# A four-layer graph network: transposed count blocks by transposing DMA transfers in place of a second matrix, and edge weights computed in slices inside attention

## The chip, the cores and the metric

The kernel runs on one core of one Trainium2 chip. The core has five engines with their own instruction streams: TensorE (PE, with its weight loads as PEld), VectorE (DVE), ScalarE (ACT), GpSimd (POOL) and SyncE (SP), which here issues DMA transfers; POOL issues the indirect ones. The metric is the device time of one launch in microseconds (us), given as the median of some runs; a profile describes one further, separately recorded execution.

## The reference

There are 3125 nodes with 256 features and 50,000 directed edges, sorted by destination. Four stages follow one another, and after each one its result is added to its input and normalized over the features (`x = layernorm(x + layer(x))`):

- Layer 0: an input projection and two transformer layers whose attention runs over the edges (8 heads of 32, softmax over the edges of each destination) with a feed-forward part of width 1024.
- Layer 1: graph attention with 4 heads of 64. An edge's weight is `exp(leaky_relu(el[src] + er[dst]))`, summed per source.
- Layer 2: two hypergraph convolutions. Each multiplies by a weight, sums over the edges from sources to destinations, divides by the destination's number of edges, and sums back from destinations to sources.
- Layer 3: messages along the edges. Each message is multiplied by four edge attributes and by a radial weight of the edge, which needs only the edge's ten length features and two small weights, nothing of the layers before:

```python
h = silu(edge_len_emb @ fc_w1 / np.sqrt(10.0)) * SILU_NORM     # 10 -> 64
msg_rad = h @ fc_w2 / np.sqrt(64.0)                            # 64 -> 1
messages = msg_ang * msg_rad
agg = segment_sum(messages, edge_dst, num_segments=n)
```

## The kernel before

Nodes are padded to NP = 3200, that is NN = 25 tiles of P = 128. Edges are laid out as NT = 391 columns of 128. The class `Sorted` holds the path that runs; a fallback for inputs that are not sorted stands in the other branch of a test and is not run.

**The count matrix.** Layers 1 and 2 don't walk over edges: they multiply by a dense 3200 x 3200 bfloat16 matrix in HBM that holds how many edges go from a source to a destination. Two of them are made. `mats[0]` has a row for each destination and a column for each source, `mats[1]` the other way round. Each is zeroed by 20 transfers of 1 MB (`clear`, L1117) and then filled by 391 indirect transfers on POOL, each writing 128 two-byte counts to places given by `put0` or `put1` (`fill`, L1131, for `mats[0]`; `fill_now`, L1138, for `mats[1]`). `count`, `put0` and `put1` are made in the prologue (`counts`); `put1` goes to HBM by L1112 and is read back in layer 1.

**Prologue** (`prepare`, from 0 to about 286 us). It finds each tile's edges, tests the order, makes the counts, and in `project_all` goes over the 25 tiles: input projection, store of h (L1272), one `clear` of `mats[0]` for each of the first 20 tiles, normalization, and query, key and value rows with their stores (L1245, L1248); the tile's edge lists (L1023, L1024, with a value read into a register of SP) come some tiles later. The radial weights of layer 3 are here too. `load_edge_weights` loads the ten features of all edges, fc_w1 six times on a diagonal, fc_w2, and the four attributes (`attr`). `edge_weights` then takes 66 steps: a float32 matmul over six groups of 128 edges (L1918, two passes on PE), Silu on ACT (L1921), a product and a sum on DVE (L1922, L1923). At the end it multiplies `attr` by the result (L1925), transposes 16 blocks (L1930), copies them (L1932) and stores them as e_w (L1933). Then `put_by` stores six tables to HBM as by_* (L1033), and the next stage begins with loading them as k_* (`fetch_by`, L1039).

**Attention** (`attend`, once for each of the two layers of layer 0; about 290 to 1226 and 1233 to 2134 us). For each tile of destinations 17 indirect gathers of key and value rows run on POOL (recorded at the helper line L996), one gather of scores (`mine`, L996) and five fills of `mats[0]`; on PE the query rows are spread over the edges (L1467), and values are summed (L1543). SP and POOL keep the order in which the code is written (the class `InOrder`). In attention layer 0 each of the first 20 tiles also issues one `clear` of `mats[1]`. Groups of GP = 3 tiles are handed to `feed`, a generator with the output, feed-forward (L1325, L1339) and next projection (L1384). Generators stand in a list `work`; `pump(n)` advances the first of them by n yields, so that feed work lies between the pieces of attention. At the end of attention layer 1, POOL issues the fills of `mats[0]` that are left.

**Layer 1** (`layer1`, 2134 to about 2765 us). For blocks of 1280, 1280 and 640 sources and two pairs of heads it loads rows of `mats[0]` as m1 (L1765), makes edge terms on ACT and DVE (L1768, L1770) and multiplies on PE (L1774). After each tile's products, `fill_now` issues four fills of `mats[1]` on POOL until all 391 are issued. After each block an epilogue (transposes L1786, DVE, ACT) normalizes and splits each float32 feature into three bfloat16 parts (`split`).

**Layer 2** (`layer2`, to about 3735 us). `conv` is called four times: with `mats[1]` and `parts` from source to destination (first and third), with `mats[0]` and `mids` back (second and fourth). A conv goes over five groups c of CT = 5 output tiles and, for each, over 25 input tiles b. For each b it loads a 128 x 640 block of the matrix as m2 (L1820, 160 KB, eight buffers), whose five 128 x 128 pieces are the weights of ten matmuls (L1825, L1827). In the first conv ACT also sums each block's rows (`tally`, L1852) for the number of edges of each source. **Layer 3** gathers rows and applies e_w to the end at 4357.7 us.

Of the kernel before, what the change touches and what calls it, by code (L numbers as in the profile page):

```python
# [8 lines left out]
F32 = mybir.dt.float32  # L9
I32 = mybir.dt.int32  # L10
# [44 lines left out]
RU = 6  # L55
LATE = 4
RS = 1280
FILL, FILL1 = 5, 4
# [944 lines left out]
class Sorted(General):  # L1003
# [58 lines left out]
    def counts(self, k, cp, sp, raw):  # L1062
# [6 lines left out]
        self.put1 = self.dram.tile([P, NT], I32, name="put1d")  # L1069
# [34 lines left out]
        back = cp.tile([P, NT], F32, name="back")  # L1104
        nc.vector.scalar_tensor_tensor(back, src, float(NP), d, op0=ALU.mult, op1=ALU.add)
        put1 = cp.tile([P, NT], I32, name="put1s")
        for c, to in ((code, self.put0), (back, put1)):
            gap = sp.tile([P, NT], F32, name="gap")
            nc.vector.tensor_sub(gap, behind, c)
            nc.vector.tensor_mul(gap, gap, away)  # L1110
            nc.vector.tensor_add(to, gap, c)
        nc.sync.dma_start(self.put1, put1)  # L1112

    def clear(self, i, z, c):

        rows = self.mats[i][:NP * NP, :].rearrange("(p c) o -> p (c o)", p=P)
        ins = self.tc.nc.sync.dma_start(rows[:, c * ZC:(c + 1) * ZC].rearrange("p (r z) -> p r z", z=ZB),  # L1117
                                        z[:, None, :].to_broadcast([P, ZC // ZB, ZB]))
        self.tc.keep_in_program_order(ins)

    def zeros(self):
        z = self.keep.tile([P, ZB], BF16, name="zmat")
        self.nc.vector.memset(z, 0.0)
        self.mats = [self.dram.tile([NP * NP + EP, 1], BF16, name=f"mat{i}") for i in range(2)]
        return z

    def fill(self, i, put, j, behind):

        tc = self.tc
        with tc.issue_after(behind.ins):  # L1130
            ins = tc.nc.gpsimd.indirect_dma_start(  # L1131
                out=self.mats[i], out_offset=bass.IndirectOffsetOnAxis(ap=put, axis=0),
                in_=self.count[:, j:j + 1], in_offset=None)
        tc.declare_no_dep(ins.ins, group=f"fill{i}", reason="each place is written once")
        tc.add_to_no_dep_group(f"fill{i}", ins.ins)

    def fill_now(self, i, put, j):
        ins = self.tc.nc.gpsimd.indirect_dma_start(  # L1138
            out=self.mats[i], out_offset=bass.IndirectOffsetOnAxis(ap=put[:, j:j + 1], axis=0),
            in_=self.count[:, j:j + 1], in_offset=None)  # L1140
        self.tc.declare_no_dep(ins.ins, group=f"fill{i}", reason="each place is written once")
        self.tc.add_to_no_dep_group(f"fill{i}", ins.ins)
# [118 lines left out]
    def project_all(self, w, xs, wi, b, z, sp, ip, pp, mp, beside):  # L1261
# [3 lines left out]
        for t in range(NN):  # L1265
# [7 lines left out]
            if t < NP * NP // P // ZC:  # L1273
                self.clear(0, z, t)
# [126 lines left out]
    def attend(self, l, qw):  # L1401
# [6 lines left out]
        with ExitStack() as at:  # L1408
# [48 lines left out]
            def scores(t):  # L1457
# [25 lines left out]
                for c in range(FILLED[l] + t * FILL, FILLED[l] + (t + 1) * FILL):  # L1483
                    self.fill(0, self.put0[:, c:c + 1], c, behind)
                if l == 0 and t < NP * NP // P // ZC:
                    self.clear(1, self.z, t)
# [80 lines left out]
            def put(t, y_p):  # L1567
# [4 lines left out]
                if len(group) == GP or t == NN - 1:  # L1572
                    work.append(self.feed(s.hs, list(group), w, nxt, sp, hp, tp, mp))
                    group.clear()
# [9 lines left out]
            for t in range(NN + 2):  # L1584
# [31 lines left out]
                for c in range(FILLED[l] + NN * FILL, FILLED[l + 1] if t == NN else 0):  # L1616
                    self.fill(0, self.put0[:, c:c + 1], c, behind_all[0])
# [10 lines left out]
                members(t + 1)  # L1628
            pump(1000)
# [27 lines left out]
    def layer0(self, qw):  # L1657
# [4 lines left out]
        for i in range(2):  # L1662
            t = self.dram.tile([CAP + P, H], F32, name=f"scores{i}")
            nc.sync.dma_start(t[CAP:, :], z)
            self.scores.append(t)
        nxt = self.attend(0, qw)
# [12 lines left out]
    def layer1(self, parts):  # L1679
# [7 lines left out]
        mat = self.mats[0][:NP * NP, :].rearrange("(d s) o -> d (s o)", s=NP)  # L1687
        with ExitStack() as at:
# [10 lines left out]
            put1 = cp.tile([P, NT], I32, name="put1")  # L1699
            nc.sync.dma_start(put1, self.put1)  # L1700
# [47 lines left out]
            fills = iter(range(0, NT, FILL1))  # L1748
            for s0 in range(0, NP, RS):
                R = min(RS, NP - s0)  # L1750
                ot = op.tile([A1, H1, RS], F32, name="ot")
                for h0 in range(0, H1, 2):
# [6 lines left out]
                    for t in range(NN):  # L1759
# [16 lines left out]
                        j = next(fills, NT)  # L1776
                        for j in range(j, min(j + FILL1, NT)):
                            self.fill_now(1, put1, j)
# [29 lines left out]
    def conv(self, mat, parts, mp, ap, seen, done):  # L1808
# [3 lines left out]
        mat = mat[:NP * NP, :].rearrange("(d s) o -> d (s o)", s=NP)  # L1812
# [419 lines left out]
```

## Time and profile before

| | us |
|---|---|
| median of three runs | 4371.66 |
| the three runs | 4358.33, 4371.66, 4374.93 |
| the profiled execution | 4359.61 |
| its span in the trace | 4357.7 |
| PE busy | 3706.8 (85%) |
| DVE busy | 2609.1 (60%) |
| POOL busy | 2406.7 (55%) |
| ACT busy | 1360.6 (31%) |

The span is what the trace covers; the profiled execution's own time is 1.9 us longer. TensorE was granted 0.911 of its clock on average. A page's slices cut the span into 40 equal parts and give each engine's busy share in tenths; the windows give the same for stretches that one chooses, in us; the waits say which engine stood for whom, with the total, the number and the longest. A line number such as L1138 is a line of the code above; a DMA queue's own instructions have SPq for SP and POOLq for POOL.

### The profile page before, as it was taken

How to read it: one execution, taken by the hardware profiler on the slowest of the kernel's cores; microseconds unless marked ns; L12 is line 12 of the kernel's file. 1: busy time of each engine (PE TensorE's matmuls, PEld its weight loads, DVE VectorE, ACT ScalarE, POOL GpSimd, SP SyncE). 2: the span in 40 equal slices, each digit the busy share in tenths (PEclk: the TensorE clock that was granted, in tenths of full speed). 3: DMA queues.
4: the chain of work that ended last, by engine and by line, in shares of the span. 5: the costliest groups of instructions: out<-in, count | busy, mean ns of one | idle time of the engine just before them, and what ended most of it. 6: DMA issues, size and time to landing. Idle time of an engine off the chain costs nothing.

```text
span 4357.7 us, 53699 instructions
## 1 busy us (share of the span) xinstructions
PE 3706.8 (85%) x18807; PEld 2534.5 (58%) x18912; DVE 2609.1 (60%) x5129; ACT 1360.6 (31%) x2336; POOL 2406.7 (55%) x2116
## 2 busy tenths in 40 slices
PE   5866888888866888878799999299999999799998
PEld 3434666666645666666433334166556655688887
DVE  6956787787647787776467768211222123566665
ACT  3720222232211223223467768355111111000000
POOL 0026777777677777777788887600000000477776
PEclk8957988998967999989799999699999999899999
DMA  7847777776266666663222222133333333233333
GB/s 177 223 151 204 210 230 214 211 218 194 67 194 183 184 191 180 184 198 111 85 76 64 70 61 60 27 90 90 94 101 89 90 105 115 75 99 100 97 99 88
DMA packets 362289, 577.13 MB, mean 132 GB/s; under 512 B 85417, under 2 KB 265380, under 8 KB 361949
## 3 DMA queue, kind: packets, MB, share of 16 engines
q1 hardware_dynamic: 246186, 286.55, 23.1%
q0 software_dynamic: 115824, 287.06, 22.6%
q8 instruction: 152, 2.49, 0.2%
q14 instruction: 127, 1.04, 0.1%
HBM read 486.46 MB, written 86.91 MB: 132 GB/s over the span
## 4 chain that ended last, share of the span: by engine, by line
PE 34%; POOL 30%; issue 9%; DVE 9%; DMA 7%; ACT 1%; SPq 1%; POOLq 0%; ACTq 0%; DVEq 0%
POOL mat L1138 13%; PE cv L1825 11%; POOL g L92 10%; PE cv L1827 6%; POOL mat L1131 4%; PE qe L1467 4%; PE mm L1339 3%; PE acc L1543 3%; POOL kv L996 3%; PE mm L1325 3%; DMA kv<-kv,k_src 3%; DMA mine<-scores,row 2%; DVE kv L1541 1%; PE w_p L1860 1%; PE mm L1384 1%
## 5 line engine op out<-in xcount | busy, mean ns | idle before, releaser
L996 POOL DMA_INDIRECT kv<-kv,k_src x850 | 843.7, 993 | 538.7 <-issue 225.6
L92 POOL DMA_INDIRECT g<-l_tab,k_src x425 | 469.9, 1106 | 1055.5 <-issue 1050.9
L1138 POOL DMA_INDIRECT mat<-k_count,put x391 | 564.3, 1443 | 119.2 <-issue 119.2
L1774 PE MATMUL acc<-e,xe 128*65 128x512 f32 (+2 forms) x1600 | 559.7, 510 | 36.9 <-DVE e L1770 21.5
L1131 POOL DMA_INDIRECT mat<-k_count,k_put x391 | 463.1, 1185 | 120.3 <-issue 112.2
L1467 PE MATMUL qe<-q,oht 128*128 128x256 bf16 x2550 | 392.7, 303 | 151.9 <-DVE kv L1469 111.0
L1770 DVE SCALAR_TENSOR_TENSOR e<-e,m 128x1280 f32<-128x1280 f32 (+1 forms) x300 | 379.2, 1268 | 168.3 <-ACT e L1768 148.6
L1543 PE MATMUL acc<-kv,oh 128*128 128x264 f32 x1700 | 441.5, 418 | 33.1 <-DVE kv L1541 32.2
L1825 PEld LDWEIGHTS <-m 128*128 128x128 bf16 x2500 | 244.8, 98 | 361.0 <-issue 75.5
L1467 PEld LDWEIGHTS <-oht 128*128 128x128 bf16 x2550 | 319.7, 146 | 228.0 <-issue 159.5
L1774 PEld LDWEIGHTS acc<-e,xe 128*65 128x65 f32 x1600 | 216.7, 141 | 368.7 <-issue 308.4
L1768 ACT ACTIVATE e<-el,l_one,fr 128x1280 f32<-128x1280 f32 (+1 forms) x300 | 380.7, 1275 | 160.6 <-PE acc L1774 159.4
L1543 PEld LDWEIGHTS acc<-kv,oh 128*128 128x128 f32 x1700 | 347.7, 209 | 110.8 <-DVE kv L1541 45.4
L1827 PE MATMUL cv<-parts,m 128*128 128x256 bf16 x1250 | 338.8, 273 | 76.5 <-DMA m<-mat 73.9
L1825 PE MATMUL cv<-mids,m 128*128 128x512 bf16 x1199 | 394.4, 379 | 10.6 <-DVE y L1847 9.7
L1825 PE MATMUL cv<-parts,m 128*128 128x512 bf16 x1196 | 396.5, 380 | 0.3
L1469 DVE TENSOR_TENSOR kv<-kv,qe 128x512 f32<-128x512 f32 (+1 forms) x450 | 285.9, 651 | 168.3 <-DMA kv<-kv,k_src 86.6
L1981 DVE TENSOR_TENSOR ws<-oh,w_n 128x512 f32<-128x512 f32 x425 | 291.7, 691 | 158.3 <-PE acc L1986 152.2
L1986 PEld LDWEIGHTS acc<-g,ws 128*128 128x128 f32 x2550 | 352.9, 192 | 22.2
L1986 PE MATMUL acc<-g,ws 128*128 128x128 f32 x2550 | 354.4, 275 | 0.0
L1827 PE MATMUL cv<-mids,m 128*128 128x256 bf16 x1250 | 338.8, 273 | 2.6
L1983 PE MATMUL acc<-g,ws 128*128 128x256 f32 x850 | 265.1, 394 | 51.2 <-DMA g<-l_tab,k_src 39.3
(296 smaller groups left out, 5259.8 us busy)
## 6 DMA issues: line engine op xcount, KB each, us to landing
m<-mat SPq DMA_DIRECT2D x550, 160.0 KB
mat<-zmat SPq DMA_DIRECT2D x40, 1000.0 KB
m<-mat SPq DMA_DIRECT2D x100, 320.0 KB
keys<-e_dst SPq DMA_DIRECT2D x50, 544.0 KB
q<-q SPq DMA_DIRECT2D x100, 192.0 KB
kv<-kv,k_src POOLq DMA_INDIRECT x850
kv<-qkv SPq DMA_DIRECT2D x50, 256.0 KB
g<-l_tab,k_src POOLq DMA_INDIRECT x425
```

The source lines that it names most:

```text
L92: return self.nc.gpsimd.indirect_dma_start(out=out, out_offset=None, in_=table, in_offset=bass.IndirectOffsetOnAxis(ap=idx, axis=0))
L996: ins = of(*args, **kw)
L1131: ins = tc.nc.gpsimd.indirect_dma_start(out=self.mats[i], out_offset=bass.IndirectOffsetOnAxis(ap=put, axis=0), in_=self.count[:, j:j + 1] ...
L1138: ins = self.tc.nc.gpsimd.indirect_dma_start(out=self.mats[i], out_offset=bass.IndirectOffsetOnAxis(ap=put[:, j:j + 1], axis=0), in_=self. ...
L1467: nc.tensor.matmul(qe[:, u, :], s.slots[:, h0 + s0 + u, :], s.q[:, k, :], start=(k == 0), stop=(k == 2))
L1543: nc.tensor.matmul(s.acc, s.oh[i][:, u, :], kv[:, u, D:], start=(h0 + u == 0), stop=(h0 + u == S - 1))
L1768: nc.scalar.activation(e[:, :R], el[:, h - h0, :R], AF.Relu, scale=fr[:, t, h:h + 1], bias=ones)
L1770: nc.vector.scalar_tensor_tensor(e[:, :R], e[:, :R], 1.0, m[:, :R], op0=ALU.add, op1=ALU.mult)
L1774: nc.tensor.matmul(accs[h, c][:, :n], xe[:, t, h, :], e[:, c:c + n], start=(t == 0), stop=(t == NN - 1))
L1825: nc.tensor.matmul(accs[i], block, parts[:, b, :2, :].rearrange("p a f -> p (a f)"), start=(b == 0), stop=False)
L1827: nc.tensor.matmul(accs[i][:, :D], block, parts[:, b, 2, :], start=False, stop=(b == NN - 1))
L1986: nc.tensor.matmul(acc1[:, m], ws[:, 1 + m, :], gb[:, 0:m + 2:m + 1, :], start=(s == 0 and m == 0), stop=(s == S - 1 and m == 2))
```

## The change

There is one matrix, `mat`, in place of two. `put1`, its store and load, the 20 clears in attention layer 0 and the 391 `fill_now` in layer 1 are gone. The first and third conv (`turned`) read `mat` transposed: for every five input tiles one `dma_start_transpose` on SP reads a 640 x 640 block (819,200 bytes) and puts it into a tile of 128 x 5 x 640, of which there are three buffers. There are 25 such transfers in a turned conv. The second and fourth conv load as before.

The radial weights leave the prologue. `load_edge_weights` loads fc_w1 and fc_w2 alone, ahead of the first attention layer. `radial` does RB = 4 of the EB = 66 steps, with its own loads of the ten features, and one such generator is put into `work` after each `feed`: 17 slices over the two attention layers. `edge_weights` with the attributes, transposes, copies and stores is a generator at the end of attention layer 1.

```diff
 def conv(self, turned, parts, mp, ap, seen, done):
...
             for b in range(NN):
-                m = mp.tile([P, CT * P], BF16, name="m2")
-                nc.sync.dma_start(m, mat[b * P:(b + 1) * P, c * CT * P:(c + 1) * CT * P])
+                if not turned:
+                    m = mp.tile([P, n], BF16, name="m2")
+                    nc.sync.dma_start(m, mat[b * P:(b + 1) * P, c * n:(c + 1) * n])
+                else:
+                    if b % CT == 0:
+                        mt = mp.tile([P, CT, n], BF16, name="m2t", bufs=3)
+                        nc.sync.dma_start_transpose(mt, mat[c * n:(c + 1) * n, b * P:b * P + n])
+                    m = mt[:, b % CT, :]
...
-                self.conv(self.mats[1], parts, mp, ap, None if n else tally, to_dst)
+                self.conv(True, parts, mp, ap, None if n else tally, to_dst)
...
-                self.conv(self.mats[0], mids, mp, ap, None, to_src)
+                self.conv(False, mids, mp, ap, None, to_src)
 # attend
-                if l == 0 and t < NP * NP // P // ZC:
-                    self.clear(1, self.z, t)
...
                     work.append(self.feed(s.hs, list(group), w, nxt, sp, hp, tp, mp))
+                    work.append(self.radial(sp, mp))
...
+            if l + 1 == LAYERS:
+                work.append(self.edge_weights(hp, sp, mp))
             pump(1000)
 # layer0
+        self.load_edge_weights(self.wp)
         nxt = self.attend(0, qw)
 # layer1
-                        j = next(fills, NT)
-                        for j in range(j, min(j + FILL1, NT)):
-                            self.fill_now(1, put1, j)
+    def radial(self, sp, mp):
+        nc, a, ew, F = self.nc, self.a, self.ew, 64
+        b0 = ew.next
+        ew.next = b1 = min(b0 + RB, EB)
+        if b0 == b1:
+            return
+        emb = sp.tile([10 * RU, RB, P], F32, name="emb", bufs=1)
+        if (RU - 1) * EB + b1 > NT:
+            nc.vector.memset(emb, 0.0)
+        for u in range(RU):
+            n = min(b1 - b0, NT - u * EB - b0)
+            if n > 0:
+                nc.sync.dma_start(emb[10 * u:10 * (u + 1), :n, :].rearrange("k b e -> k (b e)"),
+                                  a["edge_attr_10"][:, (u * EB + b0) * P:(u * EB + b0 + n) * P])
+        yield
+        for b in range(b0, b1):
+            p = mp.tile([P, 2 * D], F32, name="mm")
+            nc.tensor.matmul(p[:, :RU * F], emb[:, b - b0, :], ew.w1.rearrange("k u f -> k (u f)"),
+                             start=True, stop=True)
+            hs = sp.tile([P, RU, F], F32, name="rad_h")
+            nc.scalar.activation(hs.rearrange("p u f -> p (u f)"), p[:, :RU * F], AF.Silu,
+                                 scale=1.0 / math.sqrt(10.0))
+            nc.vector.tensor_mul(hs, hs, ew.w2[:, None, :].to_broadcast([P, RU, F]))
+            nc.vector.tensor_reduce(ew.rad[:, :, b], hs, AX.X, ALU.add)
+        yield
 # prepare
-            ew = self.load_edge_weights(cp)
...
-            self.edge_weights(cp, rs, rp, *ew)
             self.put_by()
```

The new `edge_weights` does for each chunk of 128 columns of edges what the old one did for all: load of attr, product with `rad`, four transposes, copy, store, and a yield.

## The prediction

> **What bounds the kernel now.** I read the slices of the page first, then the stages one by one with the windows, then the waits in the stages that the change touches.
>
> ```profile
> PE   5866888888866888878799999299999999799998
> ...
> POOL 0026777777677777777788887600000000477776
> ...
> DMA  7847777776266666663222222133333333233333
> ```
>
> A digit is a tenth of busy time in 109 us. No single engine sets the whole: the first two and a half slices (prologue) have no POOL work, in attention (slices 3 to 20) PE, DVE and POOL share the load, and from slice 20 on (layers 1 and 2) PE stands at 9, but for one hole, the 2 in slice 26. The hole and the prologue are where this change works. The stages by windows (columns: window, its length, busy us and instructions of PE, weight loads, DVE, ACT, POOL, then clock, DMA share, GB/s):
>
> ```profile
> 100.00:190.00 90.00, 76.61 (x255) 40.41 (x253) 87.79 (x272) 71.80 (x124) 0.00 (x0) 0.98 0.99 263
> 190.00:240.00 50.00, 42.68 (x109) 21.04 (x109) 47.18 (x135) 31.10 (x56) 0.00 (x0) 0.85 0.36 110
> 240.00:286.00 46.00, 35.22 (x65) 17.41 (x64) 28.20 (x58) 16.22 (x29) 0.69 (x1) 0.54 0.11 35
> 500.00:1100.00 600.00, 507.13 (x2649) 395.68 (x2648) 478.70 (x959) 179.33 (x330) 438.72 (x411) 0.90 0.72 213
> 1300.00:2000.00 700.00, 564.15 (x3056) 448.84 (x3056) 538.35 (x1039) 179.84 (x336) 541.34 (x501) 0.88 0.62 186
> 2160.00:2200.00 40.00, 40.00 (x112) 15.33 (x111) 25.47 (x18) 26.78 (x22) 33.91 (x21) 1.00 0.27 75
> 2745.00:2825.00 80.00, 1.44 (x12) 1.15 (x12) 16.74 (x64) 12.64 (x23) 54.65 (x57) 0.51 0.07 17
> 2900.00:3000.00 100.00, 99.34 (x586) 61.48 (x596) 12.77 (x30) 57.24 (x148) 0.00 (x0) 1.00 0.33 89
> ```
>
> Three things are to be seen. The prologue is bound by DMA and DVE until 190 and by neither after 240. Between layers 1 and 2 (2745 to 2825) only POOL works. In layer 2 PE is full at full clock, with DMA a third busy. The waits of the hole (2740 to 2830: total us, times, longest) and of SP late in the prologue (100 to 286):
>
> ```profile
> PE cv L1827 <- DMA m<-mat: 73.9, 1, 73.9
> ```
>
> ```profile
> SPq L1933 <- ACT w L1932: 45.6, 4, 43.6
> ```
>
> The row of the fills says who holds the m load back, since the first m may be read only when all 391 are done:
>
> ```profile
> L1138 POOL DMA_INDIRECT mat<-k_count,put x391 | 564.3, 1443 | 119.2 <-issue 119.2
> ```
>
> 564.3 us of work and 119.2 of issue follow one another from 2133.5 to 2817. PE is through with layer 1's products at 2742.9.
>
> **Prologue: -74.** The change takes out 66 steps of radial work. In the trace the last key and count are done by 231, the last by_ store is issued at 232.58, and then SP stands on the store of e_w (the 43.6 above) until 277.53; the first k_ load follows at 281.72, and the first gather of attention waits for it. The by_ stores need about 2 us to land, so the tail 235 to 281.72 goes: -46, and 37 of the 66 DVE pairs (L1922, L1923) stand in it. The other 29 lie before 228.5, on a DVE that is busy 153.75 of the 167 us between 62 and 229: 29 x (0.53 + 0.54) = 31. The transfers allow that much: their share in the same 167 us is 0.82, that is 137 us at full rate, less 3 for attr's 0.8 MB, so the clears and stores could end at about 196, 33 before 229. Both floors cannot be reached at once, so I take -28. What is late next is the key and count work on DVE and the last clears. Range -46 to -79. SP's seven fc loads now stand ahead of attention's first q and keys loads (at 285.58 and 286.27): about 3.3 us of SP issue, which I put at +2 in the next sum.
>
> **Attention: +15.** 17 slices of four steps enter the work list after the feeds. By the prologue's rows one slice costs DVE 4 x (0.54 + 0.54) = 4.3 us, PE eight passes at 74.1/132 = 0.56, that is 4.5, and ACT 4 x 0.49 plus up to two table loads of 1.28, that is 4.5; six small loads go on SP. A slice comes with each group of three tiles, about 101 us in attention layer 0 and 97 in layer 1. If every engine's slice were in the path of the end, the 17 would cost 17 x 4.5 = 76, plus 2: +78. If all hid, the 20 clears of mat1 that leave layer 0 (20 MB out of a DMA share of 0.72) would give something back: I take -20 as that end, about 1 us for each of the 20 tiles that had a clear, a fifth of the 4.7 to 5.2 us that a mine gather in the chain takes there. Between them: in layer 1 POOL is busy 541 of 700, with 135 of issue and 3% of waits for other engines, so it sets the pace and I charge a tenth of 8 x 4.5, 4 us. In layer 0 PE (0.85), DVE (0.80) and POOL (0.73 with 0.17 of issue) take turns, so I charge half of 9 x 4.5, 20 us, less 11 for the clears. 4 + 20 - 11 + 2 = 15. The waits that are added are of PE for the loads of a slice; they are issued one yield ahead, and what stands behind the matmul is feed work, not the gathers. The four chunks at attention's end (1.8 us DVE, 16 x 0.42 PE, 4 x 1.07 ACT, loads) lie beside the last 76 fills of mat0, which keep POOL busy to 2134 while PE has 13.4 us of work in 2110 to 2136: nothing. With that cover gone, some 30 us.
>
> **Layer 1: 0.** 391 fills leave POOL, but PE is busy 40.00 of 40.00 in the window 2160 to 2200 and waits for POOL nowhere.
>
> **The hole: -70.** As built, the first transposing transfer waits for layer 1's last product and last e, not for the epilogue, and two more follow it; so it starts at 2743. PE has transposes of the epilogue (L1786) to 2751.6. If the transfer needs 5 to 13 us from issue to landing (the first m took 4.52), PE begins at 2752 to 2757 instead of 2825.5. -73 to -68; the bad end of -60 has a landing after 2765. I take -70. The last five tiles of parts are ready at about 2764, long before the conv needs them.
>
> **Layer 2: 0, if one transfer needs under 9.1 us.** Four convs last 910 us, 227.5 each, bound by PE; 25 transfers serve one turned conv, so each may take 9.1. Bytes are the same: five 160 KB loads become one of 819,200 B. No row shows a transposing transfer, so I bound it.
> - Whole rows: in 2900 to 3000 the m loads took 32.3% of 16 x 100 us for 8.85 MB, so 819,200 B take 3.0 us.
> - Pieces of 256 B (128 columns): rows of 1280 B took 74.8 ns of an engine (517 us / 6912), rows of 2560 B in layer 1 143 ns (164 / 1152). The line through them is 0.053 ns a byte and 6.6 ns a piece: 20 ns, x 3200 / 16 = 4.1 us.
> - Pieces of 32 B: 8.3 ns x 25,600 / 16 = 13.3 us.
> - Single elements: 40 fills (2760 to 2810, 5120 elements) took 1.9% of 16 x 50 us, 3.0 ns each: x 409,600 / 16 = 76 us.
>
> I take 4.1: the nearest row is the m load itself, the same matrix, bytes and queue. The three buffers let two transfers run ahead, so that up to about 18 us of latency is covered too. The first eight m loads of the plain conv that follows are issued ahead of the transposes, 13 us of its work; the rest queue behind them on SP.
>
> The trace shows 3.0 us of transfer time for these bytes untransposed. Against this change speaks the Trainium skill, "VectorE: DVE Perf Modes", section "The three transpose paths": it lists 1309 ns for a 128x128 bf16 transpose by the DMA crossbar, and if the 25 blocks of a transfer went one after another that would be 32.7 us, two turned convs 1180 us longer, about 5410 in all (an estimate from that page). The skill's "Advanced Engine Details and Errata", section "X-Bar Transpose (TRN2)", says that transposing DMAs are as fast as ordinary ones, which would leave 0. No row here decides between the two pages.
>
> **Sum.** -74 + 15 + 0 - 70 + 0 = -129. The profiled execution took 4359.6 (span 4357.7), so 4231. It lies 12 below the median of the three runs (4371.66), inside their spread; I keep its scale. The own range of this case: 4359.6 - 79 - 20 - 73 = 4188 to 4359.6 - 46 + 40 - 60 = 4294.
>
> **Rivals.**
> - *The transfer becomes the bound of the turned convs* (slower). At the 13.3 us of 32 B pieces each turned conv lasts 332 instead of 227.5: +210, and the first transfer lands some 9 later: 4231 + 219 = 4450. It decides from 9.1 us on, and eats the whole 129 at 9.1 + 129/50 = 11.7. For it: a transpose writes each element to another partition, and small pieces cost far more per byte in the fills' row. Against it: the reads are long and DMA has 0.67 to spare.
> - *The transpose runs by block or element*, 17 to 76 us: 4231 + 2 x (425 - 227.5) = 4626 and up, to 7580. Only the fills' row, which is another queue, speaks for it.
> - *Attention pays the moved work in full*: +78 instead of 15, 4294. For it: PE 0.85 and DVE 0.80 in layer 0; against it: POOL's pace in layer 1.
> - *It doesn't do what it says*, the hole stays because the first transfer waits for the epilogue too: start at 2770, -55, 4246. The built order speaks against that; it lies in the first case's range.
>
> **How the numbers follow.** The forecast (hidden transposes) 0.62, attention in full 0.06, transfers of 9.1 to 14 us 0.16, slower ones 0.16. The range leaves out the last case and little more: 4190 to 4490 (14 us gives 4231 + 245 + 9). About 0.5% is what a measurement can tell from no change, 22 us here. Faster 0.67 (0.62 + 0.06, less a tail of 0.01), same 0.03 (transfers near 11.7 us), slower 0.30.
>
> **What would show it.** First k_ load at about 208 instead of 281.7; attention layer 0 some 10 us longer than its 936 and layer 1 about 4; PE's first conv product 9 to 14 us after layer 1's last; turned convs at 227 us with PE at 0.99 and no wait of PE for m2t. A PE that waits for m2t every five blocks, and a DMA share well over a third in the turned convs, would make the prediction wrong, and so would an SP that stands long at the transposes' issue, since the plain loads queue behind them.

## The result and the profile after

| | us |
|---|---|
| changed kernel, median of four runs | 4300.93 (4294.32 to 4303.19) |
| kernel before, median of four runs | 4365.85 (4358.33 to 4374.93) |
| ratio, 95% interval | 0.9848 (0.9823 to 0.9873) |
| span of the profiled execution | 4299.9, before 4357.7 |

The kernel is faster, by 65 us in the medians and 58 in the spans of the two profiled executions, where 129 were forecast: right in sign, about half in size. The slices of the page:

```profile
PE   5657888888757888888599998999999999799998
...
POOL 0067777777567777777500000000000000577776
...
DMA  7766566655165666664222221433334333233333
```

The 2 in PE's row at slice 26 is gone, POOL is idle through layers 1 and 2, and the prologue is shorter (POOL starts in slice 3 with a 6 and not a 2). Hardly seen at this width is where the gain of the prologue went. So I cut both traces at the same eight events; "maxima" is the reduction of a tile's gathered scores on DVE, of which there is one for each of the 2 x 25 tiles:

| stretch | before | after | difference | forecast |
|---|---|---|---|---|
| start to the first maxima (prologue) | 344.9 | 273.2 | -71.7 | -74 |
| tiles of attention layer 0 | 796.7 | 802.2 | +5.5 | } |
| seam: last maxima of layer 0 to first of layer 1 | 129.0 | 164.2 | +35.2 | } +15 |
| tiles of attention layer 1 | 760.9 | 779.9 | +19.0 | } |
| end: last maxima to layer 1's first product | 107.8 | 135.9 | +28.1 | 0 |
| layer 1's products | 603.6 | 600.6 | -3.0 | 0 |
| the hole | 82.6 | 5.9 | -76.8 | -70 |
| first conv | 230.7 | 237.5 | +6.8 | 0 |
| second to fourth conv, layer 3 | 1301.5 | 1300.5 | -1.0 | 0 |

They add up to -57.9, the difference of the spans. Hole and prologue came close to the forecast; attention and its end took back 88.

The hole in the timeline of PE (start, length, instruction, idle time before it):

```profile
2758.14 0.77 PE L1771 MATMUL r_p<-ident,ot 65*128 65x65 f32 x8 [1.36 <-DVE y L1780]
2761.84 0.61 PE L1818 MATMUL cv<-parts,m2t 128*128 128x512 bf16 x1 [2.94 <-DMA m2t<-mat]
```

Of the 73.9 us of waiting for m there are 2.94 left, for the first transposed tile. The turned convs, by the answer on their transfers' line (durations are of SP's issue, min/median/max in ns), by the third conv's window (220 us) and by the DMA in 3260 to 3400:

```profile
L1812 SPq DMA_TRANSPOSE m2t<-mat x50: 2927/3138/3892, 2756.0 to 3417.4; - x50
```

```profile
3220.00:3440.00 220.00, 219.75 (x1313) 134.69 (x1313) 27.89 (x67) 29.38 (x82) 0.00 (x0) 1.00 0.39 83
```

```profile
q1 hardware_dynamic: 48478, 12.29, 39.9%
```

12.29 MB are 15 transfers of 0.819 MB, in packets of 256 bytes (48,478 / 15 = 3232). 39.9% of 140 us of all engines, over 15, is 3.7 us for one; PE needs 9.1 us for its five blocks and is busy 219.75 of 220.

The seam, in the chain of work (start, length, what):

```profile
1151.59 1.63 DMA emb<-in_edge_attr
1153.35 5.47 PE mm L1915 x8
1158.84 0.49 ACT rad_h L1918
...
1178.60 0.32 SPq L998
...
1180.97 1.64 DMA emb<-in_edge_attr
1182.70 1.63 PE mm L1915 x2
1184.40 1.25 ACT L1918
1185.69 0.50 ACT rad_h L1918
1186.24 2.94 PE mm L1915 x4
1189.20 0.50 ACT rad_h L1918
1189.72 0.56 DVE rad_h L1920
1190.66 0.56 DVE rad L1921
1191.28 0.35 SPq L998
```

Here two whole slices lie on the path one after the other: the q store at 1149.33 or 1178.60, six issues on SP, the landing, four steps on PE and ACT, then the feed of the last tile or the next store. Each takes about 10 to 13 us where its longest engine's share had been put at 4.5. PE stands idle for the loads (the time in brackets):

```profile
1153.35 5.45 PE L1915 MATMUL mm<-fc,emb 60*128 60x384 f32 x8 [6.88 <-DMA emb<-in_edge_attr]
1182.70 2.90 PE L1915 MATMUL mm<-fc,emb 60*128 60x384 f32 x4 [5.91 <-DMA emb<-in_edge_attr]
```

No tile of the second attention layer runs beside them, since that layer's weights and first tile are loaded behind them on SP. A third slice stands ahead of these two, among the last value sums of layer 0 (its loads at 1082.71, its products from 1091.34).

The end, before: PE did layer 1's first terms (L1741) while POOL issued the last fills, and then waited.

```profile
2111.00 12.88 PE L1741 MATMUL r_p<-yt_s,l_wlb 64*128 64x512 f32 x16
2139.34 3.65 PE L1774 MATMUL acc<-e,xe 128*65 128x512 f32 x4 [15.46 <-issue]
```

After, by the waits of 2100 to 2156:

```profile
PE mm L1941 <- DVE attr L1937: 30.9, 4, 15.3
ACT w L1943 <- PE mm L1941: 30.9, 4, 15.4
DVE attr L1937 <- DMA attr<-in_edge_attr: 24.5, 3, 13.9
```

The last fill ends at 2119, but the chunks' loads, products, transposes and stores follow one another until 2144, and only then, at 2144.28, PE begins with layer 1's first terms (L1730, 11.2 us).

### The profile page after: what moved, and what is told of

The parts are those of the page before. It is cut to its first block, busy times and chain, and to the rows that moved or that the text cites. A ratio compares the mean times of both kernels' runs of the same rounds, so it can differ in the third digit from the quotient of the medians.

```text
span 4299.9 us, 53032 instructions
## 1 busy us (share of the span) xinstructions
PE 3699.6 (86%) x18912; PEld 2528.6 (59%) x18912; DVE 2609.2 (61%) x5129; ACT 1349.3 (31%) x2335; POOL 1860.9 (43%) x1725
## 4 chain that ended last, share of the span: by engine, by line
PE 47%; POOL 16%; DVE 11%; DMA 9%; issue 7%; ACT 3%; SPq 1%; POOLq 0%; DVEq 0%; ACTq 0%
PE acc L1762 11%; PE cv L1818 9%; POOL g L94 9%; PE acc L1530 5%; PE cv L1820 5%; POOL kv L998 4%; PE qe L1456 3%; PE mm L1314 3%; POOL mat L1127 3%; DMA kv<-kv,k_src 3%; PE mm L1328 3%; DMA m2t<-mat 2%; DMA g<-l_tab,k_src 1%; DVE kv L1458 1%; PE mm L1373 1%
## 5 line engine op out<-in xcount | busy, mean ns | idle before, releaser
L998 POOL DMA_INDIRECT kv<-kv,k_src x850 | 854.3, 1005 | 496.6 <-issue 227.5
L1456 PE MATMUL qe<-q,oht 128*128 128x256 bf16 x2550 | 382.1, 297 | 169.8 <-DVE kv L1458 116.4
L1530 PE MATMUL acc<-kv,oh 128*128 128x264 f32 x1700 | 451.2, 423 | 25.8 <-DVE kv L1528 25.8
L1762 PEld LDWEIGHTS acc<-e,xe 128*65 128x65 f32 x1600 | 215.0, 140 | 351.2 <-issue 289.9
L1818 PE MATMUL cv<-mids,m 128*128 128x512 bf16 x1250 | 408.4, 379 | 10.8 <-DVE y L1840 9.6
L1818 PE MATMUL cv<-parts,m2t 128*128 128x512 bf16 x1250 | 412.4, 380 | 3.2 <-DMA m2t<-mat 2.9
L1820 PE MATMUL cv<-parts,m2t 128*128 128x256 bf16 x1250 | 339.0, 273 | 0.0
L1528 DVE TENSOR_TENSOR kv<-kv 128x1536 f32<-128x1536 f32 x150 | 245.9, 1658 | 10.0 <-ACT kv L1512 10.0
L1459 DVE TENSOR_REDUCE sc<-kv 128x48 f32<-128x1536 f32 x150 | 248.6, 1657 | 0.8
```

The costliest lines, as they stand in the source:

```text
L998: ins = of(*args, **kw)
L1456: nc.tensor.matmul(qe[:, u, :], s.slots[:, h0 + s0 + u, :], s.q[:, k, :], start=(k == 0), stop=(k == 2))
L1530: nc.tensor.matmul(s.acc, s.oh[i][:, u, :], kv[:, u, D:], start=(h0 + u == 0), stop=(h0 + u == S - 1))
L1762: nc.tensor.matmul(accs[h, c][:, :n], xe[:, t, h, :], e[:, c:c + n], start=(t == 0), stop=(t == NN - 1))
L1818: nc.tensor.matmul(accs[i], block, parts[:, b, :2, :].rearrange("p a f -> p (a f)"), start=(b == 0), stop=False)
L1820: nc.tensor.matmul(accs[i][:, :D], block, parts[:, b, 2, :], start=False, stop=(b == NN - 1))
```

## The experiments

**Theory.** The moved work is dear because of where it stands: a slice or a chunk among tiles costs little, one at the seam or at the end costs its whole latency. **Rival:** it costs PE, DVE and ACT time wherever it stands (the prediction's rival "attention pays in full"), or the loss belongs to the single matrix.

### One part of the change alone

`e1_transposes_alone`: one matrix and the turned convs, radial weights in the prologue.

```diff
-                    work.append(self.radial(sp, mp))
...
-            if l + 1 == LAYERS:
-                work.append(self.edge_weights(hp, sp, mp))
...
-        self.load_edge_weights(self.wp)
... (load_edge_weights and edge_weights as before, radial gone)
 # prepare
+            ew = self.load_edge_weights(cp)
...
+            self.edge_weights(cp, rs, rp, *ew)
```

> One matrix and the turned convs as changed, the radial weights in the prologue as before. Theory 1 (the moved radial work costs attention and its two seams 88 us, more than the 72 that the prologue gives back): 16 us less than the changed kernel, about 4285, attention tile to tile as before less a few us for the missing clears, first product of layer 1 about 108 us after the last maxima of attention, hole about 6 us. Theory 2 (the moved work pays, and the loss against the forecast is something that the one matrix brings, such as the fills or the layout of the pools): about 4350 or more, with the seams as long as in the changed kernel.

Measured: 4287.31, 0.984 (0.9826 to 0.9855). Seam 130.3, end 106.8, layer 1's tiles 767.3, hole 6.0. So the single matrix does not lengthen the seams, and the transposes alone make the whole gain. Layer 0's tiles took 802.3 without clears and without slices, against 796.7 before: the missing clears gave nothing back.

`e2_radial_alone`: two matrices, clears, fills and plain convs as before, radial weights as in the change.

> Two matrices, clears, fills and plain convs as before, the radial weights moved as in the change. Theory 1: slower than before by 16 us and some 5 to 10 more, since the clears stay in attention layer 0: about 4385; prologue 72 shorter, seam between the attention layers 35 longer, end of attention 28 longer. Theory 2: faster than before by about 59, 4305.

Measured: 4355.03, 0.9986 (0.9977 to 0.9995), between the two expectations. Prologue 63.5 shorter, seam 36.7, layer 1's tiles 20.1 and the end 20.4 longer, as theory 1 has it but for a shorter end. What I had left out is the hole, which fell from 82.6 to 64.3:

```profile
PE cv L1831 <- DMA m<-mat: 55.5, 1, 55.5
```

With two matrices the hole ends when POOL has issued 391 fills, which begin after the last fill of mat0, not after layer 1's products. Layer 1 began some 20 us later after that fill, and the hole gave 18 of them back (the last fill ends at 2816.7 before and at 2816.0 here). The move by itself is worth 0.1%.

### The end and the seam one by one

`e3_m1_loads_behind`:

```diff
-                        nc.sync.dma_start(m[:, :R], mat[t * P:(t + 1) * P, s0:s0 + R])
+                        ins = nc.sync.dma_start(m[:, :R], mat[t * P:(t + 1) * P, s0:s0 + R])
+                        if s0 == h0 == 0:
+                            tc.keep_in_program_order(ins)
```

> The changed kernel, with the m1 loads of layer 1's first block kept behind the attribute loads on SP. Theory 1 (at the end of attention the second to fourth attribute load wait on SP behind m1 loads that wait for the last fill, and layer 1's first terms wait on PE behind their transposes): the chunks move under the fills and layer 1's first product comes 25 to 30 us sooner, about 4273. Rival (the fills or the loads of x set layer 1's start): less than 5 us of gain, about 4300.

Measured: 4300.14, 0.9867 (0.9851 to 0.9882), no gain that shows; the stretch from the last fill to layer 1's first product fell from 36 to 26. The expectation failed, and its timeline of PE says why:

```profile
2119.17 1.10 PE L1943 MATMUL mm<-ident,attr 128*128 128x128 f32 x4 [6.46 <-DVE attr L1939]
2125.51 1.10 PE L1943 MATMUL mm<-ident,attr 128*128 128x128 f32 x4 [5.24 <-DVE attr L1939]
2131.88 1.10 PE L1943 MATMUL mm<-ident,attr 128*128 128x128 f32 x4 [5.27 <-DVE attr L1939]
2137.09 1.01 PE L1943 MATMUL mm<-ident,attr 128*7 128x128 f32 x4 [4.10 <-DVE attr L1939]
2139.27 11.18 PE L1730 MATMUL r_p<-yt_s,l_wlb 64*128 64x512 f32 x14 [1.18 <-ACT w L1945]
```

A chunk takes 6.3 us, the next one's load waits for its buffer, and the first starts at about 2112, when the last feed is done; the fills end at 2124. The m1 loads on SP were a third of the loss, the chunks' own chain behind the feed the rest.

`e4_no_slices_at_the_seams`:

```diff
-RB = 4
+RB = 5
...
-                    work.append(self.radial(sp, mp))
+                    if t <= 20:
+                        work.append(self.radial(sp, mp))
```

> The changed kernel with slices of five steps instead of four, handed out with the first seven groups of each attention layer alone, so that none is left for the two seams. Theory 1 (what costs at the seam between the layers is slices that run when no gather, score or value work of a tile lies beside them): the seam, 164 us from the last maxima of layer 0 to the first of layer 1, falls by 25 to 35, and the total to about 4270; the tiles themselves cost up to 5 us more. Rival (the slices cost the same wherever they stand, by PE and DVE time): within 5 us of the changed kernel, 4300.

Measured: 4295.07, 0.9849 (0.9835 to 0.9864). The seam fell from 164 to 143 (the seventh slice still stood in it, from 1090 to 1108), layer 1's tiles rose to 789, the prologue took 8 us longer than in the profiled execution of the change. The end stayed at 135.0, though only a slice of one step ran there (loads at 2027.9) where the changed kernel has two slices (loads at 2030.9 and 2084.0); so it is the chunks and not the slices that lengthen the end. Seen in the seam, not in the total.

### Without the work, and all of it in layer 0

These ran on one chip with the changed kernel again, `c1_changed_again`: 4313.29, 0.9876 (0.9861 to 0.9892) of a kernel before of 4365.04.

> The changed kernel itself, as the measure for the other runs beside it on the same chip: 4301 where the kernel before takes 4360, that is 0.985 of it.

`c2_no_radial_work`: no slices, no chunks; a copy of the attributes from HBM to HBM stands in for the edge weights.

> The changed kernel without any radial work, once more, since the first time was on a chip on which the kernel before took 5897 us instead of 4360 (its edge weights are wrong numbers of the right size). Theory 1: 79 less than the changed kernel on the same chip, 4222 where that takes 4301: 35 at the seam, 28 at the end, about 15 in layer 1's tiles, nothing in layer 0's. Rival (the moved work costs its PE and DVE time in every tile): the difference lies in the tiles, 40 us or more of it, and the seams change little.

Measured: 4228.54, 0.9692 (0.9678 to 0.9706), 85 below the changed kernel beside it. Seam 130.8 against 165.4, end 106.9 against 135.9, layer 1's tiles 759.3 against 791.6, layer 0's 801.7 against 806.1: of about 100 us, 64 stand at the two seams, 32 in layer 1, 4 in layer 0. These stretches are those of the profiled executions, and c1's was the slowest of its five (4332.49): in four other profiles of kernels with this attention layer 1's tiles took 779.9 to 781.3, so 32 is the upper end there. Seam of the changed kernel (1075 to 1240) and of this one (1079 to 1210), by windows:

```profile
1075.00:1240.00 165.00, 108.58 (x420) 74.16 (x419) 69.31 (x151) 37.57 (x74) 96.53 (x97) 0.77 0.33 102
```

```profile
1079.00:1210.00 131.00, 92.92 (x391) 66.21 (x390) 56.38 (x125) 27.74 (x59) 95.51 (x97) 0.79 0.38 125
```

PE does 16 us more, and the seam is 34 longer: half of it is waiting. I cut both seams at three common events: PE's last projection for the last group of three tiles (L1373, at 1143.40 and 1135.83), its first feed product for the last tile (L1314, at 1158.74 and 1139.36), and SP's first load of keys for the next layer (1191.83 and 1160.73). The changed kernel's parts are 11.4, 11.8 and 11.7 us longer, and the rest 1.5 shorter: three slices, one in each part, at 11 to 12 us each.

`c3_all_in_layer0`: three slices after each of layer 0's first six groups, the chunks after layer 1's first group, their result written into the attribute tile.

```diff
-                    work.append(self.radial(sp, mp))
+                    if l == 0 and t <= 17:
+                        work.extend(self.radial(sp, mp) for _ in range(3))
+                    if l + 1 == LAYERS and t == 2:
+                        work.append(self.edge_weights(hp, sp, mp))
...
-            if l + 1 == LAYERS:
-                work.append(self.edge_weights(hp, sp, mp))
... (in edge_weights a yield behind the load, and attr in place of w4)
```

> All slices after the first six groups of attention layer 0, chunks after the first group of layer 1, once more beside the changed kernel. Theory 1: both seams as without radial work (130 and 107), layer 1's tiles about 767 to 772, layer 0's 802 to 835; total 4225 to 4255. Rival (PE at 0.85 in layer 0 can't take 76 us more): layer 0's tiles 850 or more, total 4270 or more.

Measured: 4319.64, 0.9886 (0.9871 to 0.9902). Seam 126.3, end 107.7, layer 1's tiles 766.6 with the chunks among them: these parts of the theory hold. Layer 0's tiles took 898, 96 more: here the rival is right. One slice in a group of three tiles costs layer 0 nothing that can be told; three cost 5.7 us each. From layer 0's first to its last maxima PE works 725.8 us here and 648.4 in c2, ACT 310.4 and 215.0: 4.6 and 5.6 for a slice (ACT's with its table loads), so here the whole price is paid. No engine is full over these 896 us; what passes the time on to the end was not found.

### The transposing transfer

`e7_plain_blocks`: `dma_start` of the same block in place of `dma_start_transpose`, so that the turned convs multiply by blocks that aren't turned.

```diff
-                        nc.sync.dma_start_transpose(mt, mat[c * n:(c + 1) * n, b * P:b * P + n])
+                        nc.sync.dma_start(mt, mat[c * n:(c + 1) * n, b * P:b * P + n].rearrange("(j p) q -> p j q", p=P))
```

> The changed kernel with the fifty transposing transfers replaced by plain transfers of the same 640 x 640 blocks, so that the two turned convs multiply by blocks that aren't transposed. If turning is hidden, as the turned convs' PE share says, within 8 us of the changed kernel (the first conv had 7 us more than before, ACT's row sums coming in bursts of five, and these stay); if the turned transfers cost time on PE's path, 10 us less or more.

On its chip the kernel before took 5896.95 (see below), so the stretches are compared: first conv 235.2 against 237.5, third 230.2 in both. Three kernels with turned transfers on its own chip (e5, e6 and e9, below) took 235.8 to 238.3 for the first conv, so turning costs PE 1 to 3 us there and nothing in the third.

`e8_three_transposes`: two more transposing transfers into an unread tile ahead of each.

```diff
+                        for _ in range(2):
+                            x = mp.tile([P, CT, n], BF16, name="m2x", bufs=2)
+                            nc.sync.dma_start_transpose(x, mat[c * n:(c + 1) * n, b * P:b * P + n])
```

> The changed kernel with each of the fifty transposing transfers issued three times, twice into a tile that nobody reads. It tells how far the transfer is from bounding the turned convs, whose five blocks take 9.1 us of PE. In the changed kernel an issue holds SP for 3.1 us and the data need about 3.7 us of all engines. If these are the prices, three need 9.4 of SP and 11.2 of DMA, and a turned conv becomes 25 x 11.2 = 280 instead of 230: about 100 us more in all, 4400. If the transfers overlap better than that, under 20 us more; if a transfer holds the DMA longer than its packets show, 200 or more.

Measured: 4442.44, 1.0171 (1.0156 to 1.0185), 129 more than the changed kernel beside it. In 2850 to 3000:

```profile
q1 hardware_dynamic: 135805, 34.43, 109.7%
```

42 transfers in 150 us, 3.6 each at 230 GB/s, with all engines full. Three take 10.7, above the 9.1 of PE; the first conv took 294.7. But SP issues almost without a pause there too (146.8 of these 150 us):

```profile
L1815 SPq DMA_TRANSPOSE m2t<-mat x50: 3075/3406/4094, 2770.6 to 3552.8; - x50
```

Three issues are 10.2 us, so whether the data or their issue sets the pace was not told apart. The second conv took 275.7, as copies issued for the third ran beside its plain loads and PE waited for these; the third, whose copies were done by then, took 230.

```profile
PE cv L1821 <- DMA m<-mat: 52.5, 20, 11.5
```

So the prediction's rival was right in kind: at about 2.5 times its cost the transfer, by its data or by its issue, would have been the bound.

### Slices off both seams

`e5_no_seams_chunks_early` (two slices for each of layer 0's first six groups, one for layer 1's first five, then the chunks), and `f1_six_groups_chunks_early` (one for each of the first six, five steps in layer 0, six in layer 1, then the chunks), both with the chunks written as in c3; `f2_slices_without_loads` and `f3_slices_without_silu` are the changed kernel with one edit each.

```diff
 # f1, attend
-                    work.append(self.radial(sp, mp))
+                    if t <= 17:
+                        work.append(self.radial(sp, mp, 6 if l else 5))
+                    if t == 17 and l + 1 == LAYERS:
+                        work.append(self.edge_weights(hp, sp, mp))
...
 # f2, radial
-        emb = sp.tile([10 * RU, RB, P], F32, name="emb", bufs=1)
+        if b0 == 0:
+            ew.emb = self.wp.tile([10 * RU, RB, P], F32, name="emb")
+        emb = ew.emb
...
-            if n > 0:
+            if b0 == 0:
 # f3, radial
-            nc.scalar.activation(hs.rearrange("p u f -> p (u f)"), p[:, :RU * F], AF.Silu,
+            nc.scalar.activation(hs.rearrange("p u f -> p (u f)"), p[:, :RU * F], AF.Copy,
```

> The changed kernel with the moved radial work kept off both seams: two slices after each of the first six groups of attention layer 0, one after each of the first five of layer 1, and the four attribute chunks right behind those. Theory 1 (the seams are what the moved work costs): from the last maxima of layer 0 to the first of layer 1 about 130 us instead of 164, from the last maxima of layer 1 to layer 1's first product about 107 instead of 136, tiles of attention layer 1 up to 20 us above the 767 of the kernel without moved work; total about 4245. Rival (the slices cost their PE and DVE time wherever they are): 4285 or more.

> The changed kernel with one slice after each of the first six groups of either attention layer (five steps each in layer 0, six in layer 1) and the attribute chunks right after the last of them, so that nothing of the radial work stands at a seam. Theory 1: layer 0's tiles about 802 as without radial work, the seam 130 instead of 165, layer 1's tiles 785 to 795, from the last maxima to layer 1's first product 107 instead of 136; the total 60 less than the changed kernel, 0.973 of the kernel before (about 4247). Rival (slices of more steps cost layer 0 as three slices per group did): layer 0's tiles 830 or more, total 4275 or more.

> The changed kernel with the features loaded once, in the first slice; all later slices compute on those, so that the edge weights are wrong numbers. If the six small loads on SP, which stand in its order ahead of the tiles' own loads and stores, are what layer 1's tiles pay for, these fall from 780 or 790 to about 765; and the seam falls by the 2.2 us of issue and 1.6 of landing of two to three slices, to about 155. If PE, ACT and DVE time is it, layer 1's tiles stay at 780 or more.

> The changed kernel with a copy in place of Silu in the slices, so that ACT loads no table for them (the edge weights are wrong numbers). If the table loads (1.28 us each, up to two for a slice and more where other functions come between the steps) are what the tiles of layer 1 pay for, they fall from 780 or 790 to about 765 and the seam by 5 or more; if not, both stay within 5 us of the changed kernel's.

The first runs of c2's and c3's kernels, `e6_no_radial_work` and `e9_all_in_layer0` ("the run before" is e5):

> The changed kernel without any radial work: no slices, no products with the attributes, a copy of the attributes from HBM to HBM in their place, so that the edge weights of layer 3 are wrong numbers of the right size. It gives the floor that a perfect hiding would reach. Theory 1: the prologue of the changed kernel and the attention of the kernel with the transposes alone, about 4222; against the changed kernel 79 less, of which 35 lie at the seam, 28 at the end and about 15 in layer 1's tiles. Rival (the prologue's gain was the larger part of the sum, the moved work is cheap): 4270 or more.

> As the run before, but all 17 slices after the first six groups of attention layer 0, three at a time, and the chunks after the first group of layer 1. Theory 1 with POOL as the pace of layer 1's tiles: they go back to about 770; layer 0's tiles, which showed no cost for seven slices, now have to show whether PE at 0.85 can take 76 us more: between 802 (it hides) and 850 (half and more is paid). Total 4225 to 4275.

The repeats of f1 to f3:

> Slices after the first six groups of each attention layer alone and the chunks right behind them, once more. On a chip with 4360 for the kernel before: layer 0's tiles 802, the seam 130, layer 1's tiles 785 to 795, the end 107, total about 4247. Rival (longer slices cost layer 0): tiles of layer 0 830 or more, total 4275 or more.

> The features loaded in the first slice alone (the edge weights are wrong numbers), once more. Loads on SP as the cost of layer 1's tiles: these fall from 780 or 790 to about 765, the seam to about 155 or less, total 4275 or less. PE, ACT and DVE as the cost: tiles of layer 1 at 780 or more, total 4290 or more.

> A copy in place of Silu (the edge weights are wrong numbers), once more. Table loads as the cost: tiles of layer 1 about 765; otherwise 780 or more and a total within 10 of the changed kernel's.

All of these, the first runs of c2's and c3's kernels, and a repeat of f1 to f3 fell on three chips where the kernel before took 5897 to 5916: e5, e6, e7 and e9 on one, f1 to f3 on the second, the repeats on the third. Totals can't be set beside those above; ratios and stretches can be set beside one another, best on one chip. The changed kernel itself was not run there; e7 and f3 have its attention (up to Silu).

| kernel | ratio | layer 0's tiles | seam | layer 1's tiles | end |
|---|---|---|---|---|---|
| e7, attention as changed | 0.9416 (0.9383 to 0.945) | 1167 | 235 | 1152 | 211 |
| e5 | 0.9247 (0.9215 to 0.928) | 1188 | 199 | 1127 | 165 |
| all in layer 0 (e9, kernel of c3) | 0.9189 (0.9155 to 0.9223) | 1203 | 196 | 1108 | 178 |
| no radial work (e6, kernel of c2) | 0.9083 (0.905 to 0.9115) | 1145 | 193 | 1081 | 176 |
| f3, without Silu | 0.9361 (0.9332 to 0.9389) | 1167 | 232 | 1142 | 212 |
| f2, without loads | 0.9092 (0.9053 to 0.9132) | 1080 | 202 | 1098 | 205 |
| f1 | 0.9132 (0.9095 to 0.917) | 1101 | 210 | 1131 | 184 |
| f3, repeat | 0.9357 (0.9334 to 0.9381) | 1172 | 232 | 1129 | 212 |
| f2, repeat | 0.9086 (0.9063 to 0.9108) | 1097 | 198 | 1090 | 205 |
| f1, repeat | 0.9135 (0.9114 to 0.9156) | 1104 | 199 | 1147 | 184 |

Beside e7 on one chip, e5 and e9 shorten both seams as theory 1 has it (199 and 196 against 235, 165 and 178 against 211), and pay 21 and 36 more in layer 0's tiles. f1 is the fastest by its ratio of those that compute all edge weights: 2.4 to 3.0% below the two with the changed kernel's attention, its interval apart from theirs. That agrees with the account only in part. Beside f3 on the same chip f1 is shorter by 22 us at the seam and 28 at the end (33 and 28 in the repeats), as theory 1 has it; but 66 (69) more come from layer 0's tiles, where it expected nothing, and layer 1's tiles, 11 shorter once, are 18 longer in the repeat. Its 4247 on the other chips was not measured and stays an expectation.

f2 shows that on these chips the features' small loads are most of what a slice costs: beside f3, layer 1's tiles fall by 44 us (39 in the repeats) and the seam by 29 (34), where the kernel without any radial work lies 61 (48) and 39 below f3, on another of the three chips. Silu's tables are at most the smaller part: f3's seam is 3 to 4 below e7's, its tiles of layer 1 10 to 23, on different chips. Whether the loads' price is SP's issue ahead of the tiles' own loads, the wait for the one `emb` buffer, or the landing was not told apart; f2 takes away all three. Nor is it shown that the loads are as dear on the chips of 4360 us. Two numbers of the changed kernel's own trace fit: from the first to the last of a slice's six loads SP takes 2.2 to 2.6 us among layer 0's tiles, which paid nothing, and 3.4 to 6.3 among layer 1's, which paid. Layer 0's tiles took 1145 without any radial work and 1080 with slices without loads, so on the slower chips some 60 us there depend on something else that stays open.

## Why the prediction was wrong

- **Prologue, -74:** right, -71.7 in the profiled execution and -62 to -67 in later ones. The first k_ load is at 207.45, forecast about 208.
- **Attention, +15:** the step that failed; tiles and seam together took 59.7. It charged "a tenth of 8 x 4.5" in layer 1 and "half of 9 x 4.5" in layer 0, "less 11 for the clears", by how full the engines are among tiles. Among tiles layer 0 paid nothing that shows (795 to 806 with single slices, 802 without) and the clears gave nothing; layer 1, where POOL's pace was to hide nine tenths, paid 13 to 32. Above all, three slices stood at the seam, for which the sum has no term: 35 there (e1 and c2: 130 without them), 11 to 12 each. The prediction had the slice's loads "issued one yield ahead" and only feed work behind its matmul; at the seam PE waits 6.9 and 5.9 us for them, and the next layer's loads stand behind on SP. The windows used were read rightly; they were windows of the wrong stretch.
- **The chunks, "nothing":** wrong by 28, close to the "some 30 us" named for the cover gone. The cover was counted from POOL's last fills; but the chunks stand behind the last feed, which ends near the fills' end, and ahead of layer 1's first terms on PE (e3).
- **Layer 1, 0:** -3.
- **The hole, -70:** -76.8. PE starts 5.9 us after layer 1's last product, as soon as the first transfer has landed; four of the epilogue's twenty transposes came after the conv's start, where all were counted ahead of it.
- **Layer 2, 0:** right for the transfer: 4.1 us by the line through two rows, 3.6 to 3.7 measured, in pieces of 256 bytes as assumed. The estimate of 32.7 us, from the 1309 ns of the Trainium skill's "VectorE: DVE Perf Modes", section "The three transpose paths", with the 25 blocks one after another, is refuted here: a block takes 0.15 us of the whole, so blocks overlap. The first conv's +6.8 was not foreseen; PE waits there 5.4 us for DVE's y, which waits for ACT, whose row sums now come five at a time.
- **Rivals:** "attention pays in full" gave 4294, near the result, but not by its mechanism, a price by engine time: layer 0's single slices were free, the seams cost more than the engines work. That 4294 is near the measured time is luck.
- **The own range of the case**, 4188 to 4294, took +40 for attention at its upper end without a working; attention and its end took 88.

## What to carry to other kernels

Work that is moved into a pipelined stage as filler has to be asked for its place at the stage's ends: at a seam, filler that was handed out last costs its latency from load to store, not its engine time. Leaving the last groups without it shortened the seam each time (e4, c3). It did not shorten the whole where the kernel before takes 4360 us: e4 took 4295 and c3 4320, and no kernel that moves the edge weights is shown to be faster than e1, which moves none of them (4287). Whether f1's placement does better there, or loads issued further ahead, is not shown. And where a wait is set by another engine's own start, as the hole was by POOL's fills, time lost ahead of it can come back there, so the price of a part alone (e2) is not its price beside the other part.

## What the hardware showed that was not expected

- A transposing transfer holds SP for 3.1 us of issue, a plain one of 160 KB for 0.33. Twenty-five in 230 us leave room; in e8, with copies among the second conv's plain loads, PE waited 52.5 us for these.
- The highest rate of transposing transfers was 230 GB/s (e8, all DMA engines full and SP issuing nearly all the time), where the Trainium skill's "DMA: Bandwidth & Descriptors", section "Latency and other measured facts", has 261 for one kernel.
- On three chips the kernel before took 5897 to 5916 us. Layer 1's products and the four convs lasted the same there (598 and 899 us in e7, 601 and 901 after); the stages in which POOL gathers took half as long again. In layer 3 of e7 DVE's idle time ahead of a product, for PE's last one, is long in one stretch and short in the next:

```profile
5012.74 0.69 DVE L1990 TENSOR_TENSOR ws<-oh,w_n 128x512 f32<-128x512 f32 x1 [2.15 <-PE acc L1995]
5015.68 0.69 DVE L1990 TENSOR_TENSOR ws<-oh,w_n 128x512 f32<-128x512 f32 x1 [2.25 <-PE acc L1995]
...
5031.71 0.69 DVE L1990 TENSOR_TENSOR ws<-oh,w_n 128x512 f32<-128x512 f32 x1 [0.41 <-PE acc L1995]
5032.81 0.69 DVE L1990 TENSOR_TENSOR ws<-oh,w_n 128x512 f32<-128x512 f32 x1 [0.41 <-PE acc L1995]
```

  DVE's instructions take 0.69 us in both; the wait for the other engine is what grows. POOL issues gathers up to 5022.7 and again from 5036.4: the waits are long beside them and for some us behind, and short after that. On the chips of 4360 us the same wait is 0.45 on average from 3900 to 4250 in the changed kernel (173 waits), where POOL issues gathers too. The cause stays open.
